# Second attention of a two-layer model: head scores on 32 rows, four side by side, in the PSUM banks of their decay sums

## The chip, the cores and the metric

The kernel runs on one core of a Trainium2 chip. The metric is the time of one execution on the device in microseconds (us). Engines are named as the profile names them: PE is TensorE's matmul, PEld its weight load, DVE is VectorE, ACT is ScalarE, POOL is GpSimd, SP is SyncE.

## The reference

Eight sequences of 512 tokens with 256 features pass through two layers. Each layer computes `x = x + attention(xn) + ffn(xn)`, with `xn` the layer norm of `x`. The first layer has causal softmax attention of 16 heads of 16 and a feed-forward of 8 experts (the best two per token) with a shared one. The second layer has a gated linear attention of 8 heads of 32 and again 8 experts, the best two per token. The change touches this second attention, whose reference is a recurrence over the tokens:

```python
h = x * jax.lax.rsqrt(jnp.mean(x * x, axis=-1, keepdims=True) + 1e-06) * norm_w
q, k, v = (heads(Wq), heads(Wk), heads(Wv))      # 8 heads of 32
q = _apply_rope(q, cos, sin)
k = _apply_rope(k, cos, sin)
beta, ig, og = (gate(Wbeta, bbeta), gate(Wig, big), gate(Wog, bog))
def step(M, inp):
    q_t, k_t, v_t, f_t, g_t, o_t = inp           # f = beta, g = ig, o = og
    M = M * f_t[..., None, None] + g_t[..., None, None] * scale * (k_t[..., :, None] * v_t[..., None, :])
    y_t = jnp.einsum('bhd,bhde->bhe', q_t, M) * o_t[..., None]
    return (M, y_t)
_, yT = jax.lax.scan(step, M0, (qT, kT, vT, fT, gT, oT))
return jnp.einsum('bld,ed->ble', y, Wout) + bout
```

## The kernel before

The kernel doesn't walk the recurrence token by token. It takes a sequence (a "block", `b`) as four chunks of 128 tokens (`c`, `NT` = 4). Inside a chunk, a token's output is a sum over earlier tokens of the chunk, weighted by the product of query and key and by the decay between the two tokens. What came before the chunk is held in a matrix state `m`. The decay is the exponential of a sum of logs of the forget gate.

The second attention runs in two parts, each a call of `attention1`: part "a" over blocks 0 to 3, at about 1064 to 1235 us of the span, and part "b" over blocks 4 to 7, from about 1757 us to the end. Between them lie the second layer's experts, in which TensorE is busy nearly throughout. They begin with loads of weights into buffers that the first part gives back. Part "a" also carries, as steps of `also`, the norm, the transposes and the routing for the experts; part "b" adds the experts' results to `x` (L476) and writes the output.

Within a part, `interleave` mixes the steps of a block (`main1`) with those of the next block's preparation (`prep1`): eight steps of scores and chunks against six of preparation. The last block of a part has no next block beside it. A tile framework puts the instructions in the order of each engine's queue and adds the waits; each engine works through its queue in that order.

Preparation of a block, `prep1`: for each chunk, `pa` and `pb` (L1282) project to queries, keys, values and gates. VectorE applies the rotation (`ra` L1297, `rb` L1300 and L1303, `qk` L1306), ScalarE makes `v` (L1307), VectorE the gate inputs `z` (L1310). After the fourth chunk, the gates: ScalarE's `e` (L1319) and `ln` (L1323), with a table load where ScalarE goes from the exponential to the logarithm (L1323) and back (L1423), VectorE's `lf`, `sig` and the products of `qk` and `v` with gates (L1333, L1338). Then the decays: `dec` on PE (L1343 to L1352), fed by a copy `lfx` on ScalarE (L1347), then `ew` and `tot` on ScalarE.

A chunk's scores, `s_scores`, on the 8 heads as two halves (`hf`) of four heads:

- `u` (L1402): eight ScalarE instructions, a triangular matrix scaled by each head's log gate.
- `qkT` (L1406): four transposes to PSUM, copied to SBUF as `qkTs` on ScalarE (L1408). Four heads of 32 fill 128 rows.
- `d` (L1412 and L1419): for a half, a mask in bf16 and the sum of logs in f32, 512 columns each, added up in one PSUM bank.
- `de` (L1423): ScalarE's exponential of it, 128x512.
- `qb` (L1426): VectorE spreads the queries of four heads over four copies of 128 columns, with zeros outside each head's own 32 rows.
- `a` (L1433): one product of keys with `qb`, on all 128 rows and 512 columns, in a PSUM bank of its own.
- `am` (L1434): VectorE's product of `a` and `de`.

A chunk's output, `s_chunk`: decayed queries `qw`, transposed (`qwT` L1449) and copied (`qwTs` L1451). Into the bank `y`, for each half, the state's product (L1454, 128 rows and columns) and then four heads' products of `v` and `am`, each to its own 32 partitions (L1458). ScalarE copies `y` to `yTs` (L1466), `po` (L1496) is the output projection, and VectorE adds it to `x` (L1499). Meanwhile `kw` (L1471) and `pm` (L1474) make the chunk's part of the state, and VectorE adds it to `m` (L1485 to L1489).

PSUM has eight banks. Before, `pa`, `pb` and `po` share 2 (tag `mm`), the transposes 2 (`tr`), `d` and `a` 2 (`da`), `y` has 1, and `pm` and `dec` 1 (`sm`).

Of the kernel before, what the change touches and what calls it, by code (L numbers as in the profile page):

```python
# [29 lines left out]
H1, HD1 = 8, 32  # L30
# [54 lines left out]
def tile_two_layers(  # L85
# [22 lines left out]
    nc = tc.nc  # L108
# [1139 lines left out]

    def prep1(b, ap, ps_mm, ps_sm, held1, places=None):

        wide = {"tag": "mm", "n": S} if places else {"tag": "sm", "n": 256}
        wcat = second["wcat"]

        def new(tag, *shape):
# [113 lines left out]
    def attention1(blocks, part, also, done, held1):  # L1370
        with tc.tile_pool(name=f"a1{part}", bufs=2) as ap, tc.tile_pool(
            name=f"a1mm{part}", bufs=2, space=PSUM
        ) as ps_mm, tc.tile_pool(name=f"a1tr{part}", bufs=2, space=PSUM) as ps_tr, tc.tile_pool(
            name=f"a1da{part}", bufs=2, space=PSUM
        ) as ps_da, tc.tile_pool(name=f"a1y{part}", bufs=1, space=PSUM) as ps_y, tc.tile_pool(
            name=f"a1sm{part}", bufs=1, space=PSUM
        ) as ps_sm:
            wout = second["wout"]
            moves = deque(also(ap, ps_mm))
            n_steps = len(blocks) * (3 * NT + 2)  # L1380
# [8 lines left out]
            def main1(b):  # L1389
# [7 lines left out]

                def s_scores(c):

                    u = ap.tile([P, H1, P], F32, tag="u", name=f"u{b}_{c}")  # L1400
                    for h in range(H1):
                        nc.scalar.activation(u[:, h, :], inc, AF.Copy, scale=lf[:, c, h : h + 1])  # L1402
# [5 lines left out]
                    nc.scalar.copy(qkT, pt)  # L1408
                    am = ap.tile([P, 2, 4, P], F32, tag="am", name=f"am{b}_{c}")
                    for hf in range(2):  # L1410
                        pd = ps_da.tile([P, 4, P], F32, tag="da", name=f"d{b}_{c}_{hf}")
                        nc.tensor.matmul(  # L1412
                            pd,
                            ident_h,
                            mask_gt.unsqueeze(1).to_broadcast([P, 4, P]),
                            start=True,
                            stop=False,
                        )
# [4 lines left out]
                        nc.scalar.activation(de, pd, AF.Exp)  # L1423

                        qb = ap.tile([P, 4, P], F32, tag="qb", name=f"qb{b}_{c}_{hf}")
                        nc.vector.tensor_tensor(  # L1426
                            qb,
                            qkT[:, hf, :].unsqueeze(1).to_broadcast([P, 4, P]),
                            blk.unsqueeze(2).to_broadcast([P, 4, P]),
                            ALU.mult,  # L1430
                        )
                        pa = ps_da.tile([P, 4, P], F32, tag="da", name=f"a{b}_{c}_{hf}")
                        nc.tensor.matmul(pa, qkT[:, 2 + hf, :], qb, start=True, stop=True)  # L1433
                        nc.vector.tensor_mul(am[:, hf], pa, de)  # L1434
                    got[c] = am

                def s_chunk(c):
                    am = got.pop(c)

                    py = ps_y.tile([P, 2, P], F32, tag="y", name=f"y{b}_{c}")  # L1440
                    if c:
                        pt = ps_tr.tile([P, 4, P], F32, tag="tr", name=f"qwT{b}_{c}")
                    if c:

                        qw = ap.tile([P, H1, HD1], F32, tag="qw", name=f"qw{b}_{c}")
# [3 lines left out]
                            nc.tensor.transpose(pt[:, hf, :], flat[:, hf * P : (hf + 1) * P], ident)  # L1449
                        qwT = ap.tile([P, 2, P], F32, tag="qwT", name=f"qwTs{b}_{c}")  # L1450
                        nc.scalar.copy(qwT, pt[:, :2, :])  # L1451
                    for hf in range(2):
                        if c:
                            nc.tensor.matmul(  # L1454
                                py[:, hf, :], m[:, hf, :], qwT[:, hf, :], start=True, stop=False
                            )
                        for h in range(4):
                            nc.tensor.matmul(  # L1458
                                py[32 * h : 32 * h + 32, hf, :],
                                v[:, c, 4 * hf + h, :],  # L1460
                                am[:, hf, h, :],
                                start=(c == 0),
                                stop=True,
                            )
# [42 lines left out]
                return steps  # L1507

            def prep(b):
                return prep1(b, ap, ps_mm, ps_sm, held1)  # L1510

            if blocks[0] not in held1:
                interleave(prep(blocks[0]), [], move)
# [8 lines left out]
    ready = {}  # L1522
# [57 lines left out]
    with tc.tile_pool(name="m1w", bufs=4) as wp, tc.tile_pool(  # L1580
# [5 lines left out]
    ) as ps_p:  # L1586
        Experts(route1, e1_d, wp, mp, None, ps_up, ps_dn, F1 // P, True).all(
            [lambda b=b: add_bout(b) for b in range(B)],
            prep1(B // 2, None, ps_p, ps_p, ready, places_of_prep()),
        )  # L1590
    attention1(list(range(B // 2, B)), "b", after, put, ready)

# [98 lines left out]
```

## Time and profile before

| | before |
|---|---|
| median of 11 runs | 1938.62 us |
| lowest and highest | 1932.32, 1943.49 us |
| profiled execution | 1935.28 us |
| its span | 1933.6 us |
| mean clock granted to TensorE | 0.971 |
| PE busy in the span | 1802.2 us, 93% |
| DVE, ACT, POOL busy | 831.0, 793.9, 403.8 us |
| `a` L1433, PE | 128 instructions, 608 ns mean |
| `d` L1419, PE | 128 instructions, 629 ns mean |
| `qb` L1426, DVE | 64 instructions, 684 ns mean |
| `am` L1434, DVE | 64 instructions, 685 ns mean |
| `de` L1423, ACT | 64 instructions, 596 ns mean |

The table's durations are those of single instructions. On TensorE consecutive instructions overlap, so the time that one takes from the engine is the distance between starts, which is shorter. An f32 product of 128 rows is recorded as two instructions, two passes over the same columns. In lines of the windows view, each engine's busy time in the stretch is given with its number of instructions, in the order PE, PEld, DVE, ACT, POOL, then the granted clock (1.00 is full speed), the DMA share and GB/s. In lines of the waits view, the engine and line that waited stand first, then what it waited for, the sum in us, how often, and the longest. In the timeline, each line has start, duration, engine and operation, and in brackets the idle time before it with what ended it. Rows of groups have the count, then the busy time, the mean ns of one, and the engine's idle time before them.

### The profile page before, as it was taken

The page shows a single profiled execution, that of the slowest core. Times are in us where ns is not written, and L with a number is a line of the kernel's source. Part 1 is how long each engine was busy: PE and PEld are TensorE (multiplying, and loading weights), DVE is VectorE, ACT ScalarE, POOL GpSimd, SP SyncE. Part 2 cuts the span into 40 slices and gives each one's busy share as a digit, 9 for nine tenths or more (in the row PEclk, how much of TensorE's full clock was granted, in tenths as well). Part 3 has the DMA queues.
Part 4 walks back from the last instruction along what each step waited for, and adds up shares of the span by engine and source line. Part 5 has one row for each costly group of instructions (what it writes and reads, how often), then busy time and mean ns, then how long its engine had stood idle before and what let it go on. Part 6 is the DMA issues. An engine that isn't in the chain of part 4 may idle for free. (4 is left out here: it accounts for less than half of the span.)

```text
span 1933.6 us, 28227 instructions
## 1 busy us (share of the span) xinstructions
PE 1802.2 (93%) x10680; PEld 1234.9 (64%) x10680; DVE 831.0 (43%) x1886; ACT 793.9 (41%) x1452; POOL 403.8 (21%) x457
## 2 busy tenths in 40 slices
PE   5988999999999999999867999999999999999898
PEld 3435665666666665665434555598888998896555
DVE  5463334444444433434585877611111111115765
ACT  2333344444335445344343465433333333335455
POOL 2015541211212212122132373011111111110000
PEclk9998999999999999999879899999999999999899
DMA  8823321756634434342341141376676776762400
GB/s 244 198 74 120 95 79 43 215 155 175 195 109 132 162 106 133 123 141 74 112 155 59 54 142 50 115 270 219 234 260 231 267 266 220 256 227 89 151 12 23
DMA packets 163687, 289.17 MB, mean 150 GB/s; under 512 B 63952, under 2 KB 134624, under 8 KB 152928
## 3 DMA queue, kind: packets, MB, share of 16 engines
q1 hardware_dynamic: 148432, 248.77, 40.4%
q0 software_dynamic: 13088, 36.07, 5.2%
q10 hardware_dynamic: 2032, 2.54, 0.4%
q8 instruction: 84, 1.38, 0.3%
q14 instruction: 51, 0.42, 0.1%
HBM read 206.78 MB, written 67.94 MB: 142 GB/s over the span
## 5 line engine op out<-in xcount | busy, mean ns | idle before, releaser
L659 PE MATMUL gup<-xgT,ew 128*128 128x256 f32 (+1 forms) x2080 | 386.1, 338 | 4.5 <-DMA ew<-in_dram 2.3
L692 PE MATMUL gdn<-ew,hgT 128*128 128x256 f32 x1640 | 376.6, 383 | 0.0
L659 PEld LDWEIGHTS gup<-xgT,ew 128*128 128x128 f32 x2080 | 331.8, 192 | 47.4 <-issue 7.6
L692 PEld LDWEIGHTS gdn<-ew,hgT 128*128 128x128 f32 x1640 | 307.9, 191 | 50.8 <-issue 11.5
L966 DVE TENSOR_REDUCE mx<-m 128x4 f32<-128x2048 f32 (+3 forms) x128 | 190.2, 1486 | 267.9 <-PE m L965 267.7
L991 ACT ACTIVATE pt<-s 128x2048 f32<-128x2048 f32 (+3 forms) x128 | 158.4, 1237 | 198.2 <-PE s L987 194.2
L719 POOL DMA_INDIRECT zd<-yo,row x144 | 140.5, 975 | 466.4 <-DVE yo L710 403.5
L993 POOL TENSOR_SCALAR_AFFINE_SELECT pt<-pt 128x512 f32<-128x512 f32 x128 | 83.9, 656 | 661.6 <-ACT pt L991 661.6
L670 ACT ACTIVATE hgT<-gup,ew 128x256 f32<-128x256 f32 (+1 forms) x376 | 133.9, 423 | 208.4 <-issue 122.5
L710 DVE SCALAR_TENSOR_TENSOR yo<-ew,way,yo 128x256 f32<-128x256 f32 x72 | 31.7, 481 | 296.8 <-ACT yo L708 296.8
L961 PE MATMUL m<-k,q 32*128 32x512 f32 (+3 forms) x1024 | 122.7, 490 | 23.9 <-ACT pt L991 19.0
L437 POOL DMA_INDIRECT xd<-xr,pos x128 | 128.3, 1002 | 47.0 <-issue 41.6
L987 PE MATMUL s<-qsh,k 32*128 32x512 f32 (+3 forms) x1024 | 113.0, 499 | 25.4 <-DVE mx L966 24.9
L991 ACT ACT_TABLE_LOAD x52 | 66.7, 1283 | 115.1 <-PE s L987 114.2
L961 PEld LDWEIGHTS m<-k,q 32*128 32x128 f32 x1024 | 48.5, 187 | 80.8 <-ACT pt L991 54.1
L987 PEld LDWEIGHTS s<-qsh,k 32*128 32x128 f32 x1024 | 43.2, 192 | 82.9 <-DVE mx L966 64.9
L1011 PE MATMUL av<-pt,vaug 128*32 128x256 f32 (+3 forms) x1024 | 89.8, 455 | 4.2 <-POOL pt L993 4.1
L1020 DVE STREAM_TRANSPOSE ou<-av 128x512 f32<-128x512 f32 x32 | 22.9, 717 | 142.3 <-PE av L1011 142.1
L708 ACT ACTIVATE yo<-gdn,way 128x256 f32<-128x256 f32 x72 | 30.2, 473 | 125.8 <-PE gdn L692 125.7
L1419 PE MATMUL d<-u,cs 128*128 128x512 f32 x128 | 69.8, 629 | 3.9 <-ACT u L1402 3.9
L1433 PE MATMUL a<-qb,qkTs 128*128 128x512 f32 x128 | 67.3, 608 | 5.6 <-DVE qb L1426 3.7
L1402 ACT ACTIVATE u<-cs,lf 128x128 f32<-128x128 f32 x224 | 72.2, 394 | 0.0
(254 smaller groups left out, 2345.5 us busy)
## 6 DMA issues: line engine op xcount, KB each, us to landing
ew<-in_dram SPq DMA_DIRECT2D x47, 2180.0 KB
ew<-in_dram SPq DMA_DIRECT2D x36, 1024.0 KB
xd<-zero SPq DMA_DIRECT2D x12, 1572.0 KB
z<-zd SPq DMA_DIRECT2D x32, 512.0 KB
xnT<-in_dram SPq DMA_DIRECT2D x22, 512.0 KB
xg<-xd SPq DMA_DIRECT2D x36, 262.0 KB
xg<-xd SPq DMA_DIRECT2D x144, 64.0 KB
xn_d<-l_xn SPq DMA_DIRECT2D x16, 512.0 KB
```

The source lines that it names most:

```text
L437: i = nc.gpsimd.indirect_dma_start(out=self.xd, out_offset=bass.IndirectOffsetOnAxis(ap=self.pos[k][:, at : at + 1], axis=0), in_=held[b][ ...
L659: nc.tensor.matmul(ps[:, j, at : at + m], wu[u][:, k, f * P : (f + 1) * P], x, start=(k == 0), stop=(k == KD - 1),)
L670: nc.scalar.activation(ht[:, f, at : at + m], ps[:, j, at : at + m], AF.Gelu, bias=w[u][2][:, f : f + 1],)
L692: nc.tensor.matmul(ps[:, t, :], ht[:, f, t * P : (t + 1) * P], wd[:, f, :], start=(f == 0), stop=(f == nf - 1),)
L719: d = nc.gpsimd.indirect_dma_start(out=self.r.zd, out_offset=bass.IndirectOffsetOnAxis(ap=row[:, s : s + 1], axis=0), in_=y[:, s, :], in_o ...
L961: nc.tensor.matmul(ps[:, h, :w], q[r, j * P : w], k[r, :w], start=True, stop=False)
L966: last["dve"] = nc.vector.tensor_reduce(mxs[n % 2][:, j, :, HD0], ps[:, :, :w], AX.X, ALU.max)
L987: nc.tensor.matmul(ps[:, h, :w], k[r, i * P : (i + 1) * P], q[r, i * P :], start=True, stop=True)
L991: nc.scalar.activation(e, ps[:, :, :w], AF.Exp, scale=0.25)
L993: last["pool"] = nc.gpsimd.affine_select(out=e[:, :, :P], in_=e[:, :, :P], pattern=[[0, 4], [1, P]], base=0, channel_multiplier=-1, compar ...
L1011: nc.tensor.matmul(ps[32 * h : 32 * h + 32, i * P :], vaugs[b % 2][:, i, c : c + 32], e[:, h, :], start=(i == 0), stop=(i == NT - 1),)
L1402: nc.scalar.activation(u[:, h, :], inc, AF.Copy, scale=lf[:, c, h : h + 1])
```

## The change

In `s_scores`, `d` and `a` of a chunk become one PSUM tile of four banks, `da`. Bank `r` belongs to the heads `r` and `r + 4`, which lie on rows 32r to 32r + 31 of the transposed queries and keys. The upper half of each bank takes the mask and the sum of logs of its two heads (256 columns, four times instead of 512 columns twice). One exponential covers the upper halves of all four banks, 128x1024. The lower halves take the scores: eight products of 32 rows and 128 columns, in two rounds of four that stand on different rows and in different banks. `qb` goes. One `am` covers 128x1024. The heads' order in `u`, `de` and `am` follows.

In `s_chunk`, the state's product of the second half moves behind the eight products of `v` and `am`; the flags that start and end the sums in the bank follow.

The PSUM banks are shared out anew: `da` takes 4 banks, one tile; the transposes 1 instead of 2, with `pm` in the second half of the tile of `qwT`; `dec` uses `mm`; the bank `sm` goes.

```diff
-    def prep1(b, ap, ps_mm, ps_sm, held1, places=None):
-        wide = {"tag": "mm", "n": S} if places else {"tag": "sm", "n": 256}
+    def prep1(b, ap, ps_mm, held1, places=None):
...
-            ps = ps_sm.tile([P, wide["n"]], F32, tag=wide["tag"], name=f"dec{b}")
+            ps = ps_mm.tile([P, S], F32, tag="mm", name=f"dec{b}")
...
-        ) as ps_mm, tc.tile_pool(name=f"a1tr{part}", bufs=2, space=PSUM) as ps_tr, tc.tile_pool(
-            name=f"a1da{part}", bufs=2, space=PSUM
-        ) as ps_da, tc.tile_pool(name=f"a1y{part}", bufs=1, space=PSUM) as ps_y, tc.tile_pool(
-            name=f"a1sm{part}", bufs=1, space=PSUM
-        ) as ps_sm:
+        ) as ps_mm, tc.tile_pool(name=f"a1tr{part}", bufs=1, space=PSUM) as ps_tr, tc.tile_pool(
+            name=f"a1da{part}", bufs=1, space=PSUM
+        ) as ps_da, tc.tile_pool(name=f"a1y{part}", bufs=1, space=PSUM) as ps_y:
...
-                    u = ap.tile([P, H1, P], F32, tag="u", name=f"u{b}_{c}")
+                    u = ap.tile([P, 4, 2, P], F32, tag="u", name=f"u{b}_{c}")
...
-                    am = ap.tile([P, 2, 4, P], F32, tag="am", name=f"am{b}_{c}")
-                    for hf in range(2):
-                        pd = ps_da.tile([P, 4, P], F32, tag="da", name=f"d{b}_{c}_{hf}")
+                    ps = ps_da.tile([P, 4, 4, P], F32, tag="da", name=f"da{b}_{c}")
+                    for r in range(4):
                         nc.tensor.matmul(
-                            pd,
+                            ps[:, r, 2:, :],
                             ident_h,
-                            mask_gt.unsqueeze(1).to_broadcast([P, 4, P]),
+                            mask_gt.unsqueeze(1).to_broadcast([P, 2, P]),
                             start=True,
                             stop=False,
                         )
-                        nc.tensor.matmul(
-                            pd, gt, u[:, 4 * hf : 4 * hf + 4, :], start=False, stop=True
-                        )
-                        de = ap.tile([P, 4, P], F32, tag="de", name=f"de{b}_{c}_{hf}")
-                        nc.scalar.activation(de, pd, AF.Exp)
-
-                        qb = ap.tile([P, 4, P], F32, tag="qb", name=f"qb{b}_{c}_{hf}")
-                        nc.vector.tensor_tensor(
-                            qb,
-                            qkT[:, hf, :].unsqueeze(1).to_broadcast([P, 4, P]),
-                            blk.unsqueeze(2).to_broadcast([P, 4, P]),
-                            ALU.mult,
-                        )
-                        pa = ps_da.tile([P, 4, P], F32, tag="da", name=f"a{b}_{c}_{hf}")
-                        nc.tensor.matmul(pa, qkT[:, 2 + hf, :], qb, start=True, stop=True)
-                        nc.vector.tensor_mul(am[:, hf], pa, de)
+                        nc.tensor.matmul(ps[:, r, 2:, :], gt, u[:, r], start=False, stop=True)
+                    de = ap.tile([P, 4, 2, P], F32, tag="de", name=f"de{b}_{c}")
+                    nc.scalar.activation(de, ps[:, :, 2:, :], AF.Exp)
+                    for hf in range(2):
+                        for r in range(4):
+                            rows = slice(32 * r, 32 * r + 32)
+                            nc.tensor.matmul(
+                                ps[:, r, hf, :],
+                                qkT[rows, 2 + hf, :],
+                                qkT[rows, hf, :],
+                                start=True,
+                                stop=True,
+                            )
+                    am = ap.tile([P, 4, 2, P], F32, tag="am", name=f"am{b}_{c}")
+                    nc.vector.tensor_mul(am, ps[:, :, :2, :], de)
...
-                    if c:
-                        pt = ps_tr.tile([P, 4, P], F32, tag="tr", name=f"qwT{b}_{c}")
+                    pt = ps_tr.tile([P, 4, P], F32, tag="tr", name=f"qwT{b}_{c}")
...
-                    for hf in range(2):
+                    def of_state(hf):
                         if c:
                             nc.tensor.matmul(
-                                py[:, hf, :], m[:, hf, :], qwT[:, hf, :], start=True, stop=False
+                                py[:, hf, :], m[:, hf, :], qwT[:, hf, :], start=hf == 0, stop=hf == 1
                             )
+
+                    of_state(0)
+                    for hf in range(2):
                         for h in range(4):
                             nc.tensor.matmul(
                                 py[32 * h : 32 * h + 32, hf, :],
                                 v[:, c, 4 * hf + h, :],
-                                am[:, hf, h, :],
-                                start=(c == 0),
-                                stop=True,
+                                am[:, h, hf, :],
+                                start=(c == 0 or hf == 1),
+                                stop=(c == 0 or hf == 0),
                             )
+                    of_state(1)
...
-                        pm = ps_sm.tile([P, 256], F32, tag="sm", name=f"pm{b}_{c}")
+                        pm = pt[:, 2:, :].rearrange("p i t -> p (i t)")
```

More of the change, by code (lines that the diff above doesn't have):

```diff
@@ L1398, in s_scores @@
                 def s_scores(c):
-                    u = ap.tile([P, H1, P], F32, tag="u", name=f"u{b}_{c}")
+                    u = ap.tile([P, 4, 2, P], F32, tag="u", name=f"u{b}_{c}")
                     for h in range(H1):
-                        nc.scalar.activation(u[:, h, :], inc, AF.Copy, scale=lf[:, c, h : h + 1])
+                        nc.scalar.activation(
+                            u[:, h % 4, h // 4, :], inc, AF.Copy, scale=lf[:, c, h : h + 1]
+                        )
                     pt = ps_tr.tile([P, 4, P], F32, tag="tr", name=f"qkT{b}_{c}")
@@ L1418, in s_scores @@
                         )
-                        nc.tensor.matmul(
-                            pd, gt, u[:, 4 * hf : 4 * hf + 4, :], start=False, stop=True
-                        )
-                        de = ap.tile([P, 4, P], F32, tag="de", name=f"de{b}_{c}_{hf}")
-                        nc.scalar.activation(de, pd, AF.Exp)
-                        qb = ap.tile([P, 4, P], F32, tag="qb", name=f"qb{b}_{c}_{hf}")
-                        nc.vector.tensor_tensor(
-                            qb,
-                            qkT[:, hf, :].unsqueeze(1).to_broadcast([P, 4, P]),
-                            blk.unsqueeze(2).to_broadcast([P, 4, P]),
-                            ALU.mult,
-                        )
-                        pa = ps_da.tile([P, 4, P], F32, tag="da", name=f"a{b}_{c}_{hf}")
-                        nc.tensor.matmul(pa, qkT[:, 2 + hf, :], qb, start=True, stop=True)
-                        nc.vector.tensor_mul(am[:, hf], pa, de)
+                        nc.tensor.matmul(ps[:, r, 2:, :], gt, u[:, r], start=False, stop=True)
[10 more added lines that the diff above has]
+                                stop=True,
+                            )
+                    am = ap.tile([P, 4, 2, P], F32, tag="am", name=f"am{b}_{c}")
+                    nc.vector.tensor_mul(am, ps[:, :, :2, :], de)
                     got[c] = am
@@ L1509, in prep @@
             def prep(b):
-                return prep1(b, ap, ps_mm, ps_sm, held1)
+                return prep1(b, ap, ps_mm, held1)
             if blocks[0] not in held1:
@@ L1588, in tile_two_layers @@
             [lambda b=b: add_bout(b) for b in range(B)],
-            prep1(B // 2, None, ps_p, ps_p, ready, places_of_prep()),
+            prep1(B // 2, None, ps_p, ready, places_of_prep()),
         )
```

## The prediction

> **What bounds the kernel now.** I read the page's busy times, then the windows of the two parts of the second attention, then TensorE's waits there, and last the timeline at one block boundary.
>
> ```profile
> PE 1802.2 (93%) x10680; PEld 1234.9 (64%) x10680; DVE 831.0 (43%) x1886; ACT 793.9 (41%) x1452; POOL 403.8 (21%) x457
> ...
> 1064.00:1235.00 171.00, 159.51 (x809) 91.68 (x810) 128.62 (x299) 92.86 (x242) 75.12 (x75) 0.97 0.21 70
> 1757.00:1934.00 177.00, 160.77 (x789) 91.43 (x787) 122.45 (x247) 91.64 (x238) 1.36 (x2) 0.94 0.22 73
> ```
>
> TensorE fills 160 us of each attention part, VectorE 129 and 122. So TensorE sets the pace, and what stops it is the next question:
>
> ```profile
> PE pb L1282 <- DVE z L1310: 2.4, 1, 2.4
> PE y L1454 <- ACT qwTs L1451: 1.9, 1, 1.9
> PE a L1433 <- DVE qb L1426: 1.8, 1, 1.8
> ```
>
> These are the largest three waits of the first part but for `po` on `yTs` (2.5 in four); the second part has two like them (`qwTs` 1.9, `qb` 1.9), 1.8 on `qkTs` and 2.6 on `u`. Counting idle stretches over 0.1 us, TensorE stands 14.4 us in the first part and 11.2 in the second: little to win, much to lose if each of 32 chunks gets a new wait. The boundary between blocks, on PE and then on ACT:
>
> ```profile
> 1150.40 1.07 PE L1433 MATMUL a<-qb,qkTs 128*128 128x512 f32 x2
> ...
> 1151.97 0.38 PE L1449 MATMUL qwT<-cs,qw 128*128 128x128 f32 x2
> 1154.22 0.49 PE L1454 MATMUL y<-qwTs,m 128*128 128x128 f32 x2 [1.87 <-ACT qwTs L1451]
> 1154.64 0.43 PE L1458 MATMUL y<-am,v 128*32 128x128 f32 x8
> 1154.99 0.49 PE L1454 MATMUL y<-qwTs,m 128*128 128x128 f32 x2
> 1155.41 0.43 PE L1458 MATMUL y<-am,v 128*32 128x128 f32 x8
> 1155.77 0.39 PE L1412 MATMUL d<-mask_gt,ident_h 128*128 128x512 bf16 x1
> ```
>
> ```profile
> 1149.37 0.28 ACT L1319 ACTIVATE e<-e 128x96 f32<-128x96 f32 x1
> 1149.67 1.28 ACT L1323 ACT_TABLE_LOAD   x1
> 1150.96 0.23 ACT L1323 ACTIVATE ln<-den 128x32 f32<-128x32 f32 x1
> 1151.21 1.28 ACT L1423 ACT_TABLE_LOAD   x1
> 1152.50 0.60 ACT L1423 ACTIVATE de<-d 128x512 f32<-128x512 f32 x1
> ```
>
> PE durations overlap in this view, so I cost by starts. The next block's `ln` puts two table loads on ScalarE; `de` and `qwTs` queue behind them and `y` waits 1.87 us.
>
> **TensorE work removed.** A half's product is two passes 0.43 us apart, 0.86 us; a chunk's two cost 1.72. The new form has a model in the first attention, four heads side by side on 32 rows at 128 columns:
>
> ```profile
> 501.12 0.50 PE L987 MATMUL s<-qsh,k 32*128 32x128 f32 x8
> 501.55 0.70 PE L659 MATMUL gup<-xgT,ew 128*128 128x256 f32 x2
> ```
>
> Eight records are four matmuls of two passes, 0.43 us. Eight products: 0.86, and 0.10 to enter the tiling (`y` starts 0.20 us after the last `state` pass, where plain passes follow at 0.11). I take 0.96, saving 0.76 a chunk; the ends are 0.53 (the second four wholly beside the first) and 1.76 (nothing side by side, eight at the 0.22 of a plain 128-column pair). The `y` stretch, 1154.22 to 1155.77, is 1.55; without the return into tiling between halves it is 0.42 (`state`) + 0.71 (two `y` sets at 0.36) + 0.22 = 1.35: 0.20 less, in 24 chunks. Masks and sums move the same columns in twice as many instructions: nothing, at most four further weight loads of 0.05 where one isn't hidden. In all 32 × 0.76 + 24 × 0.20 = 29.1 us less TensorE work, 3.64 per block.
>
> The Trainium skill ("TensorE: Matmul & The Clock Gate", Measured speedup vs the span model) has four row tiles at 512 columns 3.07 times faster than in turn. By that figure as an estimate the products would cost 1.76 / 3.07 = 0.57, and the forecast would fall by about 10 us; no run here shows it at 512 columns in turn, and the row above stands.
>
> **Other engines.**
>
> ```profile
> L1434 DVE TENSOR_TENSOR am<-a,de 128x512 f32<-128x512 f32 x64 | 43.9, 685 | 33.9 <-PE a L1433 30.8 <-ACT de L1423 3.1
> L1426 DVE TENSOR_TENSOR qb<-qkTs,cs 128x512 f32<-128x512 f32 x64 | 42.4, 684 | 14.2 <-ACT qkTs L1408 14.2
> L991 ACT ACTIVATE pt<-s 128x1024 f32<-128x1024 f32 x32 | 32.8, 1024 | 51.5 <-PE s L987 51.4
> ```
>
> VectorE loses `qb`, 42.4 us; `am` becomes 32 of 1.22 (as L1338's 128x1024, 1217 ns), 39 against 43.9. ScalarE's `de` becomes 32 of 1.02: 32.8 against 38.2. All this lies beside TensorE, so it pays only where TensorE waits for VectorE.
>
> **Waits added.** Sums and products now share the four banks of one tile, and there is one such tile. In the changed program's order the first product waits for `de` in all 32 chunks, and the next chunk's first mask for `am`. The trace has no such pair on one bank. If the wait were not there, the price below for it is nil; if it is, it is the exp's whole duration. I take the whole. Per block that is not a part's last, PE gaps:
> - Chunk 2: sums end, 0.2 latency, `de` 1.02, 0.15 back: 1.37; only `qwT` (0.22) is queued between. +1.15.
> - Chunk 3: `e` runs 2.70 us after the last `pa` pass ended (1146.67) and the second load ends 5.82 after it. `pb` 0.95, `qkT` 0.44, sums and masks 2.05 put the sums' end 3.44 after that `pa`; so `de` ends 3.4 after the sums, the products start at 3.57, and TensorE idles 3.35 instead of 1.87: +1.48. Before, `a` was already computed here.
> - `po` of chunk 2: `yTs` is queued behind `lfx` (0.61) and eight `u` (2.45 at 0.305); it lands at 7.4 after the sums' end where TensorE is ready at 6.3: +1.04.
> - First masks of chunks 1 and 2 wait for `am`, which VectorE has behind `ra`, `rb`, `rb`, `qk` of the next block: 2.35 + 1.22 + latency = 3.92 after `pa`, against 3.2 of TensorE work in between: +0.7 twice, 1.45.
> - Smaller `yTs` and `qwTs` waits: +0.5.
>
> Sum 5.6, less 3.64 of work: a clean block gets 2.0 us longer.
>
> **The clock.** After a stall, stretches of 3.4 us at half clock appear:
>
> ```profile
> 1846.60:1850.00 3.40, 1.54 (x17) 0.98 (x17) 2.60 (x6) 3.39 (x9) 0.00 (x0) 1.00 0.00 0
> 1850.02:1853.42 3.40, 3.40 (x14) 1.67 (x15) 1.98 (x5) 1.74 (x6) 0.00 (x0) 0.50 0.00 0
> ```
>
> TensorE was busy 1.54 of 3.40, with 1.86 idle, and the next 3.4 us ran at 0.50. The like 1.87 at 1152.35 drew none. A 3.35 us gap should always draw one: up to 1.7 us lost, less what the queued waits hide; I take 1.0 a block.
>
> The Trainium skill (same page, Part 1: The HAM clock gate) puts the throttle after a whole idle window of about 3.4 us. By that the clock term would be 0 and the forecast 6 us lower; the rows above throttled at 1.86, so the measurement decides.
>
> **The sum.** Blocks are told by the start of the last `po`: the four steady ones take 41.04, 44.97, 46.82, 42.98, together 175.8. A clean one becomes 41.04 + 2.0 + 1.0 = 44.0, so 176.2 in all; the three slower ones exceed 41.04 by 11.7, 1.0 of it clock already counted, and I keep half of the remaining 10.7, since VectorE's delays there (additions of 1.24 us, `qk` beside GpSimd) now delay `am`: +5.7. The parts' last blocks (28.34 and 27.11) have nothing of a next block to fill waits: they become a chain of masks and sums 2.05, `de` 1.37, products 0.96, `am` 1.22 + 0.35 = 5.95 a chunk. First sums and `po` 2.4, then 3.9 to the second mask, two chunks more (12.2), sums with `qkT` 2.5, and 8.1 through the tail: 29.1, and 0.5 of clock. That is +1.2 and +2.5, 3.7. The first blocks: in the first part the stretch 1080 to 1100 is VectorE's (19.84 of 20 busy), which gains 2.0 or so, against the boundary's +5.6 + 1.0 − 3.64 + 0.5: +1.5; in the second part, `qb` and `qkTs` waits (1.91, 1.84) and the half clock after them go in part: −2.5. Together 5.7 + 3.7 − 1.0 = +8.4; experts between are shifted, not changed, as their weight loads wait for the attention's buffers. The profiled execution was 1935.28 (span 1933.6): 1943.7; the median of runs lies 3.3 higher, 1938.62: **1946**.
>
> **Rivals.**
> - *Faster: the short waits close.* If `am` and `yTs` are served in time, the masks' 1.45 and `po`'s 1.04 fall out of six blocks: −15, total −6.6, median 1932. It decides when a block's new waits stay under 3.6 less the clock's 1.0. For it: VectorE is 47 us lighter. Against: the queues stand in that order in every block. 0.14.
> - *VectorE's relief is worth its full price.* `qb` waits 1.75, 1.91, 0.69, `qkTs` 1.84, and the half clock around 1795 and 1806: a further −6 to −8, about +1, median 1939 to 1940, inside what a measurement here can tell from no change (0.2%, ±3.9 us). 0.16.
> - *The rows don't run side by side*: products 1.76, 0.8 more in some 26 uncovered chunks, +21: 1967. Against: L987's row. 0.10; or more clock and `am` waits, +5 to +14 above the forecast, 1951 to 1960: 0.15.
> - Forecast, 1942.5 to 1951: 0.45.
>
> So faster 0.14, same 0.16, slower 0.70. Range 1933 to 1961: it leaves out the unpacked case and the best of the first rival.
>
> **What would show it.** Right: products of eight records in about 0.96 us; a wait of `da` on `de` of 1.1 us in chunks 2 and of over 3 at six boundaries; 0.50 windows after those; `qb` gone from the waits. Wrong: first product right behind the sums; boundary gaps near 1.9; TensorE's idle time in both parts (25.6 now) below about 50; last blocks under 27 us.

## The result and the profile after

The changed kernel takes 1940.9 us (median of 17 runs) where the kernel before, in the same runs, takes 1934.5 (63 runs): ratio 1.0042, interval 1.0031 to 1.0054. The ratio is that of the means (1943.6 and 1935.4 us), or 8 us slower; the medians lie 6.4 us apart. The profiled execution of the changed kernel took 1952.6 us, 17.3 more than that of before; it is one of the longest of the 19 on record, which run from 1932.7 to 1953.7, so its profile shows more loss than the usual execution has. Of the 17.3 us, 6.7 lie in the first layer, which the change doesn't touch: the half-clock stretch that begins at 771.4 us in one trace begins at 778.1 in the other. I read the attention's stretches by themselves, each from its first transposes (`qkT`) to its last `po`, start to start: the first part took 164.96 us and takes 177.09, the second took 172.89 and takes 172.39; together 337.9 and 349.5.

The page's busy times and the windows of the two parts (columns as before):

```profile
PE 1783.6 (91%) x11256; PEld 1261.9 (65%) x11256; DVE 785.9 (40%) x1790; ACT 790.1 (41%) x1420; POOL 399.4 (20%) x457
...
1070.70:1252.30 181.60, 155.08 (x1096) 108.93 (x1097) 104.73 (x250) 91.24 (x226) 72.58 (x75) 0.89 0.20 66
1772.50:1949.50 177.00, 146.81 (x1085) 102.25 (x1083) 102.27 (x201) 90.78 (x224) 1.94 (x2) 0.93 0.23 74
```

TensorE and VectorE both have less to do: 160 us and 129 of VectorE's became 155 and 105 in the first part, 161 and 122 became 147 and 102 in the second. No engine got fuller, and yet the parts aren't shorter. The clock column says a part of why: 0.97 became 0.89 in the first part.

TensorE's waits, the first two lines of the first part and then the first two of the second:

```profile
PE da L1423 <- ACT de L1419: 13.4, 8, 3.1
PE da L1410 <- DVE am L1431: 2.8, 6, 0.8
```

```profile
PE da L1423 <- ACT de L1419: 11.4, 8, 3.1
PE da L1410 <- DVE am L1431: 3.9, 5, 1.2
```

Products (`da` L1423) waiting for the exponential (`de`), 24.8 us in 16 places, stand at the top of both; the waits on `qb` are gone. The boundary between two blocks, on PE and then on ACT:

```profile
1164.62 0.38 PE L1445 MATMUL qwT<-cs,qw 128*128 128x128 f32 x2
1168.09 1.23 PE L1423 MATMUL da<-qkTs 32*128 32x128 f32 x16 [3.09 <-ACT de L1419]
1169.26 0.80 PE L1450 MATMUL y<-qwTs,m 128*128 128x128 f32 x2
```

```profile
1163.88 0.28 ACT L1317 ACTIVATE e<-e 128x96 f32<-128x96 f32 x1 [0.48 <-DVE e L1316]
1164.18 1.28 ACT L1321 ACT_TABLE_LOAD   x1
1165.47 0.23 ACT L1321 ACTIVATE ln<-den 128x32 f32<-128x32 f32 x1
1165.72 1.28 ACT L1419 ACT_TABLE_LOAD   x1
1167.02 1.02 ACT L1419 ACTIVATE de<-da 128x1024 f32<-128x1024 f32 x1
```

The last sums start at 1164.19. The exponential that the products need comes behind two table loads, and TensorE stands 3.09 us where it stood 1.87. Five of the six boundaries have this stall; at the first of the second part three shorter ones (0.96, 1.07, 0.70) stand in its place. The same eight products have stretches of 0.66 us where nothing delays them (here, in a last block, from 1932.36 to 1933.02), and the `y` stretch ahead of them takes 1.22 (1930.83 to 1932.05); the lines of L1474 are `pm`, which now lies in the tile of `qwT`:

```profile
1930.83 0.39 PE L1450 MATMUL y<-qwTs,m 128*128 128x128 f32 x2
1931.15 0.64 PE L1457 MATMUL y<-am,v 128*32 128x128 f32 x16
1931.72 0.49 PE L1450 MATMUL y<-qwTs,m 128*128 128x128 f32 x2
1932.05 0.39 PE L1474 MATMUL qwT<-v,kw 128*128 128x128 f32 x2
1932.36 0.73 PE L1423 MATMUL da<-qkTs 32*128 32x128 f32 x16
1933.02 0.49 PE L1474 MATMUL qwT<-v,kw 128*128 128x128 f32 x2
```

At the boundary above the products took 1.17 instead (1168.09 to 1169.26): the stretch after the stall runs at half clock, as its window shows (span, five busy times with counts, clock, DMA share, GB/s):

```profile
1167.25:1174.00 6.75, 5.91 (x44) 4.78 (x45) 4.59 (x6) 5.74 (x17) 5.53 (x7) 0.50 0.42 151
```

A small account helps to read the experiments. Over both parts, the table splits the time into idle stretches of TensorE over 0.1 us and the rest; the last column is the time at half clock, in stretches counted whole where they touch a part.

| profiled execution | both parts | TensorE idle | the rest | at half clock |
|---|---|---|---|---|
| before | 337.9 | 21.2 | 316.7 | 30.7 |
| changed | 349.5 | 50.5 | 299.0 | 64.9 |
| changed, no table loads | 321.1 | 41.5 | 279.6 | 17.1 |
| before, no table loads | 324.0 | 15.0 | 309.0 | 10.2 |

The two lower rows (their edit is told below) are the cleanest comparison, since they have little half clock: the change takes 29.4 us of work from TensorE (up to 3.4 more, if the 6.9 us more at half clock are allowed for) and adds 26.5 us of idle time. The upper rows have the same trade with the loads: idle time +29.3, and 34 us more at half clock, which costs up to half of that.

### The profile page after: what moved, and what is told of

Read it like the earlier page. It is cut to its first block, busy times and chain, and to the rows that moved or that the text cites. A ratio compares the mean times of both kernels' runs of the same rounds, so it can differ in the third digit from the quotient of the medians.

```text
span 1950.6 us, 29241 instructions
## 1 busy us (share of the span) xinstructions
PE 1783.6 (91%) x11256; PEld 1261.9 (65%) x11256; DVE 785.9 (40%) x1790; ACT 790.1 (41%) x1420; POOL 399.4 (20%) x457
## 5 line engine op out<-in xcount | busy, mean ns | idle before, releaser
L1417 PE MATMUL da<-u,cs 128*128 128x256 f32 x256 | 84.1, 429 | 7.0 <-ACT u L1399 7.0
L1280 PE MATMUL pa<-wcat,xnT 128*128 128x512 f32 x128 | 64.8, 624 | 3.6 <-DVE xnT L1308 0.9
```

The lines of the kernel that those rows point to most:

```text
L1280: nc.tensor.matmul(ps[:, : c1 - c0], xnT[b][:, k, t * P : (t + 1) * P], wcat[:, k, c0:c1], start=(k == 0), stop=(k == KD - 1),)
L1417: nc.tensor.matmul(ps[:, r, 2:, :], gt, u[:, r], start=False, stop=True)
```

## The experiments

My theory: the change's saving on TensorE is eaten by products that wait for the exponential on the banks that they share with it, above all at the block boundaries, where the exponential stands behind two table loads and the stall draws half clock. The rivals: fewer buffers in PSUM (one for the transposes, one tile of scores); packed products that aren't cheaper; waits that only move when the products' one is taken away.

Eight of the runs were made on two chips on which the kernel before takes 1995 us instead of 1935: in the first block of the first part TensorE, VectorE and ScalarE stand together, TensorE up to 34.2 us at a time, in every kernel profiled there, and by different amounts. For these runs I also give the second part's time, which has no such stalls (172.9 before, 172.4 changed, in the first profiles). They are all but four: the two without loads, the products ahead without loads, and the new order of `y` in the kernel before.

**The changed kernel again.** No edit.

> The changed kernel again, for its ratio on this chip and a second profile. My theory, from the waits in its first profile: ratio 1.003 to 1.005; again 3.1 us before the products at six boundaries, 0.9 in the third chunks, and last blocks of 27.8 where no half clock falls into them, 29.4 where one does.

Ratio 1.0092 (1.0061 to 1.0123), above what I expected, on a chip where the first block holds those stalls. What the waits say came again: the second part took 172.4 us, to the tenth as in the first profile, the longest stall before products was 3.1 us, and the last blocks were 29.4. So the other runs on these chips are compared with 1.0092, not with 1.0042. Only the runs of one bank for the transposes and of the logarithm on VectorE share its chip; for the four on the other chip, where the changed kernel wasn't run, 1.0092 is borrowed. The profile's view of waits in that part:

```profile
PE da L1423 <- ACT de L1419: 11.4, 8, 3.1
PE da L1410 <- DVE am L1431: 3.9, 5, 1.2
PE da L1417 <- ACT u L1399: 3.5, 1, 3.5
```

**No table loads, changed kernel and kernel before.** Both leave the logarithm out.

```diff
-            nc.scalar.activation(ln, den[:, :, :H1], AF.Ln)
+            nc.scalar.activation(ln, den[:, :, :H1], AF.Exp)
```

> The changed kernel with the gates' logarithm replaced by an exponential (the gate values are then not the reference's), so that ScalarE has no table loads at the block boundaries in the second attention; the engines' orders are otherwise nearly the same. My theory (the largest single piece of what the change adds is the products behind the exponential behind two table loads): the six boundary gaps fall from 3.1 to about 0.9 and the half clock after them goes: 6 x (2.2 + 1.5) = 22 us less than the changed kernel, ratio to the kernel before 0.993. Rival (the waits inside chunks on the shared banks decide, the boundary is one stall like others): 6 x 1.3 = 8 us less, ratio 1.000.

> The kernel before with the same replacement of the logarithm (the gate values are not the reference's). Before, only the second half's exponential and qwTs stand behind the loads: the 1.9 us waits of y on qwTs go at the three or four boundaries that have one, with a half-clock stretch or two: 8 us, ratio 0.996. My theory: so with the loads gone the changed kernel (0.993) is ahead of the kernel before (0.996); the rival: it stays behind by about the 8 us that it is behind with them.

Both ran at 0.9924 (0.9907 to 0.9941, and 0.9910 to 0.9938). Against their own versions with loads that is 22.8 us less for the changed kernel, as expected, and 14.7 less for the kernel before, more than expected. So the changed kernel loses 8 us more to the loads than the kernel before, and that is its whole loss. In the account above the loads add only 2.8 us to the idle time that the change brings (29.3 with them, 26.5 without); the rest goes with the clock. It doesn't win without them, as I had thought it would: the two are level to about 4 us. The waits of the changed kernel without loads, second part, one boundary there, and the waits of the kernel before without loads in that part:

```profile
PE da L1423 <- ACT de L1419: 7.1, 8, 1.0
PE da L1410 <- DVE am L1431: 3.9, 5, 1.2
PE po L1496 <- ACT yTs L1466: 3.5, 4, 1.4
```

```profile
1875.92 0.38 PE L1445 MATMUL qwT<-cs,qw 128*128 128x128 f32 x2
1877.26 0.73 PE L1423 MATMUL da<-qkTs 32*128 32x128 f32 x16 [0.95 <-ACT de L1419]
```

```profile
PE d L1419 <- ACT u L1402: 2.6, 1, 2.6
PE a L1433 <- DVE qb L1426: 1.9, 1, 1.9
PE po L1496 <- ACT yTs L1466: 1.3, 3, 0.5
```

The stall of 3.09 is now 0.95, the exponential itself, in the third and fourth chunks of a block. In the kernel before without loads no wait of `y` on `qwTs` is left in that part. In the account above, the parts of the changed kernel fall by 28.4 us; 9.0 of that are idle time, and time at half clock falls from 64.9 to 17.1 us: the larger piece is clock.

**Products ahead of the sums.** Two edits together: the products stand before the masks and sums, and a chunk's transposes are issued at the end of the chunk before it. The first run has the loads, the second not.

```diff
+                    for hf in range(2):
+                        for r in range(4):
...                      # the eight products
                     for r in range(4):
...                      # masks and sums
-                    for hf in range(2):
-                        for r in range(4):
...
                     got[c] = am
+                    if c + 1 < NT:
+                        turned_qk[c + 1] = turn_qk(c + 1)
```

> As the kernel with transposes one chunk ahead, and the eight products stand before the masks and sums, so that no product waits for the exponential of its own chunk. As scheduled, ScalarE has lfx and seven or eight u between the two table loads, so the exponential of the fourth chunk and qwTs come later at the boundary. My theory: 18 waits of 0.7 to 0.9 us of products on the exponential go (-13 us), but the boundary's y waits about 6 us for qwTs instead of 3.1 (6 x 3 = +18, and clock): ratio about 1.007, with no wait of a product on the exponential left in the trace. Rival (the products' wait isn't what costs): those waits turn into others at the same places inside chunks and the ratio stays at 1.004.

> Products ahead of masks and sums, transposes one chunk ahead, and the logarithm replaced by an exponential (gate values not the reference's): neither loads nor the chunk's own exponential stand before the products. My theory: beside the changed kernel without loads, the waits of 0.9 in chunks 2 and 3 and of 0.7 to 0.9 in the last blocks go, some 14 us, against new waits of qwT and y of up to 1.1 in the chunks where the transposes' single bank holds them: between 0 and 10 us less than it, ratio about 0.990. Rival (the wait only moves: in a chunk the exponential has to end before am, and am before y, whatever the order): the same as without loads, 0.993 or above.

With loads 1.0188 (1.0157 to 1.0219), without 1.0055 (1.0035 to 1.0074): the first is above what theory and rival expected. The second is 25 us slower than the changed kernel without loads, where I expected up to 10 us faster: my theory was wrong here, and the rival right that the wait only moves, but not that the time stays the same. With the loads, the wait of `y` on `qwTs` at four boundaries is 4.7 us (I had put about 6). The waits of the run without loads, second part, first three lines, and ScalarE at one boundary:

```profile
PE y L1458 <- ACT qwTs L1455: 13.4, 12, 2.6
PE qwT L1453 <- ACT qkTs L1402: 4.6, 4, 1.2
PE pa L1280 <- DVE rb L1301: 3.8, 1, 3.8
```

```profile
1848.76 0.98 ACT L1410 ACTIVATE u<-cs,lf 128x128 f32<-128x128 f32 x3
1849.65 1.00 ACT L1435 ACTIVATE de<-da 128x1024 f32<-128x1024 f32 x1
1850.55 0.35 ACT L1455 COPY qwTs<-qwT 128x256 f32<-128x256 f32 x1
```

No product waits for `de` any more. But ScalarE still runs the exponential before the copy `qwTs`, so the stall goes to `y`, and with one bank for the transposes `qwT` waits for the copy of the next chunk's `qkT`. Idle time grows by only 4.5 us over both parts (46.0 against 41.5), but half clock from 17.1 to 51.2 us, which can cost up to 17 of the 25. The last blocks show it: 35.2 us instead of 27.7, of which 1.6 are idle time, while 9 us run at half clock and none did before. The exponential of 1.0 us is in a chain that each chunk has to go through; the order on TensorE decides which instruction shows the wait, and where the clock falls.

**Transposes a chunk ahead alone.** The second of the two edits.

> The changed kernel with one edit: a chunk's four transposes and their copy are issued at the end of the scores of the chunk before (within a block). As scheduled, ScalarE then runs the fourth chunk's exponential and the copy qwTs ahead of the table load for the logarithm, and the load back to the exponential stands before ew. Sums, exponential and products keep their order on the shared banks. My theory (the change loses by waits behind the exponential, above all the 3.1 us at six block boundaries and the half clock after them): boundary gaps fall from 3.1 to about 0.9, 6 x (2.2 + 1.2 of clock) = 20 us less than the changed kernel: ratio to the kernel before about 0.994. Rival (the loss comes from fewer buffers in PSUM, or from products that aren't cheaper): the ratio stays at 1.004; one transposes' bank with transposes issued earlier may even cost more.

Ratio 1.0017 (0.9994 to 1.0040), against 1.0092 of the changed kernel on another chip of the same sort: 15 us, between theory and rival; the second part alone took 166.0 us, 6.4 less than with the transposes in place, 2.8 of it idle time, and with 10 us less at half clock. The first part doesn't agree: its three later blocks took 124.5 us against 118.8 of the changed kernel run again, with 27 us at half clock against 14, and the profiled execution (2011.9 us) is one of the longest of this kernel, whose median is 1999.1. The stall of 3.08 went, but left two behind it: products 0.96 on `de`, `y` 1.07 on `qwTs`:

```profile
PE da L1429 <- ACT de L1425: 7.4, 9, 1.0
PE y L1458 <- ACT qwTs L1455: 6.3, 8, 1.2
```

So by the medians bringing the exponential ahead of the loads pays, as the theory says, but of 3.08 us of stall about 2 stay.

**The order in y**, in the changed kernel (old order back) and in the kernel before (new order alone).

```diff
-                    of_state(0)
-                    for hf in range(2):
+                    for hf in range(2):
+                        of_state(hf)
                         for h in range(4):
...
-                    of_state(1)
```

> The changed kernel with the order of the kernel before in y: state, four heads, state, four heads. My sum has this part at 0.20 us in 24 chunks: 4.8 us slower than the changed kernel, ratio 1.0067. Rival (the stretch is hidden by waits that follow it, for yTs or am): no change, 1.004.

> The kernel before with the change's order in y alone (state, eight heads, state). The run with the old order in the changed kernel put this part at 1 us or so, not the 4.8 of my sum: here TensorE has few waits that could hide it, so between 1 and 5 us less: ratio 0.9975 to 0.9995.

The kernel before with the new order ran at 0.9980 (0.9966 to 0.9995): 3.9 us less, the one piece of the change that pays for itself, and of the versions that leave nothing out the only one here that beats both kernels. In the changed kernel the old order gave 1.0047 (1.0027 to 1.0066), not slower at all than the borrowed 1.0092; the second part took 167.6 us, 4.8 less than the changed kernel's. But it also had 10.2 us at half clock there where the changed kernel had 23.9, and half of that difference is more than the whole effect. Where the stalls set the pace, the order in `y` can't be told from where the clock's stretches fall.

**VectorE's padded queries put back**, into a buffer that nobody reads.

```diff
+                    for hf in range(2):
+                        qb = ap.tile([P, 4, P], F32, tag="qb", name=f"qb{b}_{c}_{hf}")
+                        nc.vector.tensor_tensor(
+                            qb,
+                            qkT[:, hf, :].unsqueeze(1).to_broadcast([P, 4, P]),
+                            blk.unsqueeze(2).to_broadcast([P, 4, P]),
+                            ALU.mult,
+                        )
```

> The changed kernel with VectorE's 64 products qb put back, into a buffer that nobody reads: 42.4 us of VectorE, nothing on TensorE. My theory (VectorE's relief carries a part of the change's gain, as am stands behind VectorE's queue in the first two chunks of a block): the two waits of the first mask on am in six blocks (0.4 and 0.5) grow by up to 1.37 each, 16 us, and some more in the blocks where routing and additions fill VectorE: ratio about 1.014. Rival (VectorE is off the path): 1.004 to 1.005.

Ratio 1.0105 (1.0078 to 1.0132), within the interval of the changed kernel's 1.0092 on the other chip, and 172.7 us in the second part against 172.4. VectorE's 42.4 us are worth nothing that can be measured there: the rival was right. For the first block of the first part, where VectorE was fullest, it isn't shown: the stalls of these chips hide it, and the two ratios leave some 8 us open. The scheduler laid the queues out anew for this kernel, so the waits differ in place; their sum hardly does (25.0 us of idle time in the second part against 26.5).

**One bank for the transposes in the kernel before**, with `pm` in its second half.

> The kernel before with one PSUM bank for the transposes instead of two and pm in its second half, as the change has it; nothing else. My theory (the banks' new shares cost little; what costs is the exponential and the loads ahead of the products): transposes of the next chunk wait for copies that are long done, ratio 0.999 to 1.002. Rival (the loss of a buffer is what the change pays with): the changed kernel's whole +8 us, ratio 1.004.

Ratio 1.0074 (1.0048 to 1.0100), above both expectations; but the second part took 172.4 us, as the kernel before did in its first profile (172.9). TensorE's waits in it:

```profile
PE y L1453 <- ACT qwTs L1450: 3.9, 6, 0.8
PE qkT L1406 <- ACT qkTs L1408: 1.5, 1, 1.5
PE qwT L1448 <- ACT qkTs L1408: 0.7, 1, 0.7
```

The kernel before had 1.9 on `qwTs` and 1.8 on `qkTs` there, 2.4 us less on the two; and the second part had 10 us at half clock where that of the kernel before had 20, so an equal time can hide up to 5 us of cost. In the first part the last block took 33.6 us instead of 28.3, but 4.7 of that are `pa` and `pb` of the preparation, which the kernel before had done by then. No profile of the kernel before exists from a chip with those stalls, so I can't say which of the 15 us are the bank's. How much the smaller share of banks costs stays open; that rival isn't ruled out as a part of what the change pays.

**The logarithm on VectorE**: a series in e / (2 + e) in place of ScalarE's logarithm, nine operations on 128x32; in the changed kernel, and in the kernel before with the new order in `y`.

```diff
-            nc.scalar.activation(ln, den[:, :, :H1], AF.Ln)
+            nc.vector.tensor_scalar(lp, e8, 2.0, 0.5, ALU.add, ALU.mult)
+            nc.vector.reciprocal(lp, lp)
+            nc.vector.tensor_tensor(lw, e8, lp, ALU.mult)
+            nc.vector.tensor_tensor(lp, lw, lw, ALU.mult)
+            nc.vector.tensor_scalar(ln, lp, 1.0 / 2304, 0.0, ALU.mult, ALU.add)
+            for a in (1.0 / 448, 1.0 / 80, 1.0 / 12):
+                nc.vector.scalar_tensor_tensor(ln, ln, a, lp, ALU.add, ALU.mult)
+            nc.vector.scalar_tensor_tensor(ln, ln, 1.0, lw, ALU.add, ALU.mult)
```

> The changed kernel with the gates' logarithm computed on VectorE (a series in e/(2+e) of nine small operations on 128x32), so that ScalarE stays with the exponential's table in the second attention and all results are kept. My theory: near the run that left the logarithm out, 0.9924, plus up to 1.5 us of VectorE in 8 blocks where the gates' chain is late: ratio 0.993 to 0.998, faster than both kernels. Rival (the chain of gates on VectorE takes the place of the loads): 1.000 or more.

> The kernel before with the same series for the logarithm and the change's order in y; scores as before, with padded queries. My theory: without the loads the change's scores win nothing and lose nothing (0.9924 both), so this has the y order's 2 to 4 us on top and VectorE, which still has qb, takes the series worse: ratio 0.991 to 0.997. Rival (the packed scores pay once the loads are gone): it ends behind the changed kernel with the series by 0.002 or more.

The changed kernel with the series ran at 1.0025 (1.0005 to 1.0045), 13 us less than the changed kernel on the same chip, and its second part took 165.7 us, 6.7 less; the longest wait of a product is 1.0, as without loads. Against the kernel before it missed my 0.993 to 0.998; the rival's number, 1.000 or more, is the one that came. The second kernel ran at 1.0007 (0.9989 to 1.0024), above my range too, second part 163.8. So the loads can be taken out without leaving the logarithm out, the packed scores don't pay then either, and neither kernel beat the one before on that chip. New in its place are waits for the logs:

```profile
PE da L1433 <- ACT de L1429: 7.1, 8, 1.0
PE dec L1351 <- DVE lf L1332: 3.6, 1, 3.6
```

## Why the prediction was right

I forecast 7.4 us over the median that I had, with 0.70 for slower; measured were 8 (ratio 1.0042). The terms of my sum add up to +8.4, which on that median makes 1947, not the 1946 that I wrote.

That the total came so close is in part luck. I had +5.7 for the four steady blocks, +3.7 for the last ones and −1.0 for the first ones; in the traces they are −1.3, +3.4 and +9.6, in an execution of the changed kernel that is 12 us longer than the median. The mechanism held: new waits behind the exponential at the named places, and a loss of clock behind them. By its steps:

**Work off TensorE: right in the sum, off in the terms.** Forecast 29.1 us; the two kernels without loads differ by 29.4. But eight products take 0.66 us, not 0.96: near my lower end, where the second four lie mostly beside the first. The `y` stretch takes 1.22, not 1.35. By these numbers the saving would be 32 × 1.06 + 24 × 0.33 = 42 us. Some 8 of the other 13 were given back by neighbours: in a clean block without loads the time between starts grew by 0.25 us for `pa`, 0.3 for `pb` and 0.5 for `qwT` with `pm`, beside which the products now stand, 1.05 in each block. That this is the return from the tiling (from products of 32 rows to those of 128) is argued from where it occurs, not shown. The Trainium skill's figure ("TensorE: Matmul & The Clock Gate", Measured speedup vs the span model), by which I had estimated 0.57, was nearer to the measured 0.66 than my 0.96.

**The waits: right in place, each a little large.** Boundary stall 3.09 (forecast 3.35); third chunk 0.90 (1.15); the masks on `am` 0.39 and 0.47 (0.7 each); `po` on `yTs` 0.79 where it shows (1.04). They were too large by about 0.25. A part of that is the latency that I put behind an exponential: at the boundary shown, the products start 0.05 us after `de` ends (1168.04 to 1168.09), where I had 0.15; the rest I haven't traced. To price the wait at the exponential's whole duration was right: the products started when it had ended. The sign that I had set for TensorE's idle time, below about 50 us in both parts, was only just not met: it is 50.5, by the count that gives 21.2 for the kernel before.

**The clock: the term that was mis-sized.** I took 1.0 us a block, 7 in all with the last blocks. At or within 6 us after the six boundaries of the trace lie 3.4, 6.8, 6.8, 3.4, 3.4 and 3.4 us at half clock, 27 in all, and over both parts there are 34 us more than before. Half of that is 17, which the waits hide in part: 349.5 − 337.9 = 11.6 = −29.4 + 29.3 + 11.7, if the work is taken from the kernels without loads. So it was about 12 rather than 7. The two errors, idle time forecast too large and clock too small, nearly cancelled.

The executions say the same without a profile. Of the changed kernel's 19, the shortest (1932.7 us) has a mean granted clock of 0.973 over the whole execution and the longest (1953.7) 0.961, with the others in about that order. The kernel before, in the 16 executions listed beside the runs without loads, has a median of 1934.7 us and a clock of 0.970 to 0.976. Where the clocks are equal, so are the times, to a few us: at 0.971 to 0.973 the changed kernel has 1932.7, 1935.5 and 1938.6 us, the kernel before 1932.2 to 1938.9. So work saved and idle time added are about level, and what is left of the loss is clock.

As to the rule of the Trainium skill that I had weighed there, that the throttle comes after a whole idle window ("TensorE: Matmul & The Clock Gate", Part 1: The HAM clock gate): by it these stalls of 3.09 us would have cost no clock. A half-clock stretch came with or within 1.2 us after three of the five, and 5.6 and 5.7 us after the other two, behind another stall of 0.79 us.

**Blocks.** Steady blocks of the first part: 44.33 and 44.35 (forecast 44.0 for a clean one); of the second, 41.74 and 44.08, so my extra 5.7 for disturbances in the kernel before was not to be seen. The last blocks: 29.41 twice (29.1 and 0.5). The first block of the first part was missed most: 59.0 against 50.6, +8.4 where I had +1.5; 20.5 us of it ran at half clock, where the kernel before had 5.6, and the changed kernel without loads 11.1 in 52.5 us. 13.7 us of these stretches follow stalls at the start of the part that I had not priced: 3.5 us ahead of the block and 2.1 at the routing (`rank` on `rt_both`).

**VectorE.** I had counted 2 to 4 us of gains where VectorE was full. With `qb` put back nothing measurable was lost in the second part, so there was nothing to gain there.

The rivals: that the short waits close was wrong (they are all there), and so was the unpacked case (0.66). What the theory of the experiments had too bright: with the loads gone, the change should have won, and it only drew level.

## What to carry to other kernels

Packing products onto rows of the array saves TensorE time, but a layout that makes them share PSUM banks with an operand of ScalarE puts the exponential between two TensorE steps that were independent before. (That the shared tile forces the wait is read from the order of the trace; no run gave the products banks of their own.) Count the exponential, and whatever stands ahead of it in ScalarE's queue, against the saving. Before forecasting a gain on the engine that sets the pace, sum the idle time that the new order adds at each place in its queue, and add the clock that stalls cost afterwards: in the two traces here all but one of the stalls of 1.84 us and more in these parts were followed by a half-clock stretch, and so were some pairs of shorter ones. Reordering one engine moves such a wait to the next instruction in the chain unless something independent is put into the gap.

## What the hardware showed that I had not expected

- Eight row-packed products of 128 columns took 0.66 us, where one set of four took 0.43 in the first layer: the second set added 0.23.
- A stall of 3.09 us was followed by one half-clock stretch of 3.4 us at three boundaries and by two in a row at two others, though TensorE was busy 5.91 of 6.75 us in the one shown. Two stalls of 0.68 and 0.77 us inside 3.4 us, in each part's last block, were followed by one as well; one of 1.87 in the kernel before was not. No threshold can be read from these.
- 42.4 us of VectorE work put back on its queue in both parts changed nothing measurable in the second (172.7 against 172.4 us), though VectorE is busy 58% of it in the changed kernel.
- On two chips TensorE, VectorE and ScalarE stood together several times, TensorE for up to 34 us, in the block where the indirect transfers run, while GpSimd issued one such transfer every 1.27 us; ScalarE's line there names no engine of this core:

```profile
1122.31 0.37 ACT L1466 COPY yTs<-y 128x256 f32<-128x256 f32 x1 [6.78 <-remote]
1141.46 0.47 ACT L1305 ACTIVATE v<-pb,rms 128x256 f32<-128x256 f32 x1 [18.77 <-remote]
1140.69 0.96 POOL L437 DMA_INDIRECT xd<-xr,pos  x1 [0.30 <-issue]
```

Two such waits of the changed kernel run again, and one of GpSimd's transfers during the second. Their cause was not looked into.
